# Two attention layers in fp32: layer 0 by half rows again, and an opening that loads the pair ahead of most of x

## The chip, the cores and the metric

The kernel runs on one core of a Trainium2 chip. The metric is the device time of one execution, in microseconds. The profile is of one execution of the kernel before, with a span of 3475.1 us. The engines are named as in the profile: PE (TensorE, matmuls), PEld (its weight loads), DVE (VectorE), ACT (ScalarE), POOL (GpSimd), SP (SyncE, which only issues transfers here).

## The reference, cut to what matters

x has 128 rows of 256 tokens with 256 channels. Both layers add attention to x, computed from a group-normalized x (32 groups, statistics over all rows and tokens). Layer 0 has 8 heads of 32 channels, adds a bias made from `pair` after the softmax, and multiplies by a gate. Layer 1 has 4 heads of 64 channels and sees a band of 16 tokens to each side.

```python
def layer0(x, pair, gate_proj, qkv_proj, out_proj, bias_proj):     # x: (1, 128, 256, 256)
    bias = einsum('nijz,zh->nhij', pair, bias_proj)[:, None]       # pair: (1, 256, 256, 128)
    gate = sigmoid(x @ gate_proj)
    q, k, v = split(x @ qkv_proj, 3)                               # 8 heads of 32
    sim = softmax(einsum('nsqhc,nskhc->nshqk', q, k) / sqrt(32)) + bias
    return (einsum('nshqk,nskhc->nsqhc', sim, v) * gate) @ out_proj

def layer1(x, w_in, b_in, w_out, b_out):
    q, k, v = split(x @ w_in.T + b_in, 3)                          # 4 heads of 64
    scores = where(|i - j| <= 16, q k^T / sqrt(64), -inf)
    return softmax(scores) @ v @ w_out.T + b_out

x = x + layer0(groupnorm(x), ...)
x = x + layer1(groupnorm(x), ...)
```

The statistics of the first group norm need the whole of x, so layer 0 cannot start before x has been read once. Those of the second need all of layer 0's result.

## The kernel before

All is fp32. It has three parts: an opening (weights, the bias from `pair`, the statistics of x), layer 0 row by row, and layer 1 row by row. A branch at the end recomputes everything in a slower way if a sum of exponentials was out of range; with these inputs it isn't taken.

The opening. The weights are issued on ScalarE's queue. Layer 1's weights (`w_nat`, one transfer for each of 12 blocks and one for `w_out`) are turned by TensorE ahead of everything else. Then 32 steps m, each on half a tile of `pair` (16 tiles of 2 MB, three buffers): `turn_pair` transposes it on TensorE and copies it out, `weigh_pair` multiplies it by the bias weights, `place_bias` turns the result back into `bias_sb`. x comes in parts of 4 MB (the last two of 3 and 1 MB) in two buffers; DVE counts each with 32 `bn_stats`, one for a group.

```python
for a in range(A):
    nc.scalar.dma_start(out=qkv_sb[strip(a)], in_=by_strip(qkv_w)[a])
    nc.scalar.dma_start(out=gate_sb[strip(a)], in_=by_strip(gate_w)[a])
# ... out_sb, bqk, bv, bo and the 13 transfers of w_nat alike ...
for o4 in range(2):                      # layer 1's weights, turned
    for kt in range(2):
        pw = proj_bank(...)
        for j in range(4):
            nc.tensor.transpose(pw[...], w_nat[...], ident)
        # ... nc.scalar.copy into w_in_t, w_out_t ...

steps = NM // (NX - 1)                   # NM = 32, NX = 9
for m in range(NM):
    if m % (IC // 16) == 0:
        load_pair(m // (IC // 16))       # on SyncE's queue
    turn_pair(m)
    if m >= 1: weigh_pair(m - 1)
    if m >= 2: place_bias(m - 2)
    n, k = divmod(m, steps)
    if n >= 1:
        x_stats(stats, xss[n - 1], n - 1, range(k * G // steps, (k + 1) * G // steps))
    if k == steps - 1 and n < NX - 2:
        xss[n] = x_load(xs_pool, x[0], n, "0_")   # on SyncE's queue
# ...
for n in range(NX - 2, NX):
    x_stats(stats, x_load(xs_pool, x[0], n, "0_"), n)
mean0, rstd0 = group_columns(...)
```

Layer 0. A row s has two halves of four heads. `scores` makes the four `sim` banks of a half, their exponentials `ex` and the sums over the two key tiles `both`. `piece(s, n)` normalizes a row (n = 0) or projects q, k, v or the gate (n = 1 to 4). `attend` handles all eight heads at once, between the two halves of the next row's scores. PSUM has five shared banks, and one each for zs, bv and av.

```python
def attend(s):
    # zs: sums of the exponentials, as rows of `ones`; bv: bias times v; av: ex times v
    for half, both in enumerate((both0, both1)):
        for j in range(4):
            nc.tensor.matmul(zs[D0 * j : D0 * (j + 1), half, :], lhsT=ones[:, 0:D0], rhs=both[:, j, :], ...)
    for to, weights in ((bv0, bias), (av, ex)):
        for half in range(2):
            for kt in range(2):
                for j in range(4):
                    nc.tensor.matmul(to[D0 * j : D0 * (j + 1), half, :], lhsT=v[...], rhs=weights(h, kt), ...)
    nc.scalar.activation(z, zs, AF.Identity, accum_out=zsum[:, s : s + 1])
    nc.vector.scalar_tensor_tensor(d, st[s]["e"], 1.0, z, op0=ALU.add, op1=ALU.mult)
    nc.vector.tensor_tensor(t, bv0, z, ALU.mult)
    nc.vector.tensor_tensor(t, av, t, ALU.add)
    nc.vector.reciprocal(d, d)
    nc.vector.tensor_tensor(at, t, d, ALU.mult)
    nc.vector.tensor_reduce(zmin[:, s : s + 1], z, axis=AX.XY, op=ALU.min)

def finish(s):
    po = by_channel(out_sb, 0, st[s]["at"], ...)         # 8 PE instructions
    nc.vector.tensor_tensor(o[:, k], po, st[s]["xt"], ALU.add)
    # every second row: bn_stats for layer 1; every SG = 4 rows: store to x1

for s in range(S + 1):
    if s < S: scores(s, 0)
    attend(s - 1)
    if s < S: scores(s, 1)
    for n in range(1, 5): piece(s + 1, n)
    finish(s - 1)
    piece(s + 2, 0)
```

An fp32 matmul is two PE instructions; `by_channel` and `by_token` (q, k, v, gate, out) are four matmuls of 128 x 128 by 256 columns each. Layer 1 has the same frame with its own shapes and isn't touched.

Of the kernel before, what the change touches and what calls it, by code (L numbers as in the profile page):

```python
# [9 lines left out]
F32 = mybir.dt.float32  # L10
AF = mybir.ActivationFunctionType
ALU = mybir.AluOpType
# [22 lines left out]
def conv_preact_kernel(  # L35
# [19 lines left out]
    dram = ctx.enter_context(tc.tile_pool(name="dram", bufs=1, space=bass.MemoryType.DRAM))  # L55


    ring = {}

    def psum(scope, name, proj, sim):  # L60

        pool = scope.enter_context(tc.tile_pool(name=f"ps_{name}", bufs=1, space=PSUM))
        ring["proj"] = (pool, "proj", proj)
        ring["sim"] = (pool, "sim", sim) if sim else ring["proj"]
        return pool

    def bank(which, name):
        pool, tag, bufs = ring[which]
        return pool.tile([P, 2, R], F32, tag=tag, name=name, bufs=bufs)

    def proj_bank(name):
        return bank("proj", name)

    def sim_bank(name):
        return bank("sim", name)
# [19 lines left out]
    def strip(a):  # L95
        return slice(B * a, B * (a + 1))
# [3 lines left out]
    for a in range(A):  # L100
        nc.scalar.dma_start(out=qkv_sb[strip(a)], in_=by_strip(qkv_w)[a])
        nc.scalar.dma_start(out=gate_sb[strip(a)], in_=by_strip(gate_w)[a])
    out_sb = const.tile([P, 2, C], F32, name="out_sb")
    for kt in range(2):
        for h in range(2):
            nc.scalar.dma_start(
                out=out_sb[:, kt, h * P : (h + 1) * P].rearrange("p (a r) -> p a r", a=A),
                in_=out_w.rearrange("(t p) (a h r) -> t h p a r", p=P, a=A, h=2)[kt, h],
            )
    bqk = const.tile([P, 4], F32, name="bqk")  # L110
    with nc.allow_non_contiguous_dma(reason="512 biases, once"):
        nc.scalar.dma_start(out=bqk, in_=b_in[0 : 2 * C].rearrange("(t p) -> p t", p=P))

    bv = const.tile([P, P], F32, name="bv")
    for half in range(2):
        nc.scalar.dma_start(
            out=bv[KB * half : KB * (half + 1), :],
            in_=b_in[2 * C + P * half : 2 * C + P * (half + 1)].partition_broadcast(KB),
        )
    bo = const.tile([P, 2], F32, name="bo")  # L120
    with nc.allow_non_contiguous_dma(reason="256 biases, once"):
        for a in range(A):
            nc.scalar.dma_start(out=bo[strip(a)], in_=b_out.rearrange("(a h r) -> a r h", a=A, h=2)[a])
# [31 lines left out]
    zmin = const.tile([P, 2 * S], F32, name="zmin")  # L155
    zsum = const.tile([P, 2 * S], F32, name="zsum")
# [98 lines left out]
    with ExitStack() as early:  # L255
        ps_av = psum(early, "early", 2, 4)
# [5 lines left out]
        for t in range(6):  # L262
            for h in range(2):
                nc.scalar.dma_start(
                    out=w_nat[:, t, h * P : (h + 1) * P].rearrange("p (a r) -> p a r", a=A),
                    in_=w_in.rearrange("(t p) (a h r) -> t h p a r", p=P, a=A, h=2)[t, h],
                )
        nc.scalar.dma_start(out=w_nat[:, 6:8, :], in_=w_out.rearrange("(t p) c -> p t c", p=P))
        for o4 in range(2):
            for kt in range(2):  # L270
                pw = proj_bank(f"pw{o4}_{kt}").rearrange("p a b -> p (a b)")
                for j in range(4):
                    nc.tensor.transpose(
                        pw[:, j * P : (j + 1) * P], w_nat[:, 4 * o4 + j, kt * P : (kt + 1) * P], ident
                    )
                if o4 == 0:
                    nc.scalar.copy(w_in_t[:, kt, 0:512], pw)
                else:
                    nc.scalar.copy(w_in_t[:, kt, 512:768], pw[:, 0:256])
                    for h in range(2):  # L280
                        nc.scalar.copy(
                            w_out_t[:, kt, h * P : (h + 1) * P].rearrange("p (a r) -> p a r", a=A),
                            pw[:, 256:512].rearrange("p (a h r) -> p h a r", a=A, h=2)[:, h],
                        )

# [56 lines left out]
        steps = NM // (NX - 1)  # L342
        xss = {}
        for m in range(NM):
            if m % (IC // 16) == 0:
                load_pair(m // (IC // 16))
            turn_pair(m)
            if m >= 1:
                weigh_pair(m - 1)
            if m >= 2:  # L350
                place_bias(m - 2)
            n, k = divmod(m, steps)
            if n >= 1:
                x_stats(stats, xss[n - 1], n - 1, range(k * G // steps, (k + 1) * G // steps))
            if k == steps - 1 and n < NX - 2:
                xss[n] = x_load(xs_pool, x[0], n, "0_")
        weigh_pair(NM - 1)
        place_bias(NM - 2)
        place_bias(NM - 1)
        for n in range(NX - 2, NX):  # L360
            x_stats(stats, x_load(xs_pool, x[0], n, "0_"), n)
# [29 lines left out]
    def by_channel(w, col, xn, name, ring="proj"):  # L391

        ps = bank(ring, name)
# [20 lines left out]
    SG = min(4, S)  # L414
# [8 lines left out]
    with ExitStack() as lay:  # L423
        st1 = lay.enter_context(tc.tile_pool(name="st1", bufs=1))
        stats1 = st1.tile([P, 2, S // 2, 6], F32, name="stats1")
        with ExitStack() as lay0:
            ps_av = psum(lay0, "0", 5, 0)
# [38 lines left out]
            def scores(s, half):  # L466
# [10 lines left out]
                ex = att.tile([P, 4, 2, R], F32, tag="ex", name=f"ex{s}_{half}", bufs=3)  # L477
                for j in range(4):
                    nc.scalar.activation(ex[:, j], sims[j], AF.Exp, scale=1.0 / math.sqrt(D0))  # L479
                both = att.tile([P, 4, R], F32, tag="both", name=f"both{s}_{half}", bufs=3)  # L480
# [4 lines left out]
            def attend(s):  # L485
                if s < 0:
                    return
                (ex0, both0), (ex1, both1) = hd.pop((s, 0)), hd.pop((s, 1))
                v = st[s]["v"]

                zs = ps_av.tile([P, 2, R], F32, tag="z", name=f"zs{s}")
                bv0 = ps_av.tile([P, 2, R], F32, tag="bv", name=f"bv{s}")
                av = ps_av.tile([P, 2, R], F32, tag="av", name=f"av{s}")
                for half, both in enumerate((both0, both1)):
                    for j in range(4):
                        nc.tensor.matmul(
                            zs[D0 * j : D0 * (j + 1), half, :], lhsT=ones[:, 0:D0], rhs=both[:, j, :],
                            start=True, stop=True,
                        )
                for to, weights in (  # L500
                    (bv0, lambda h, kt: bias_sb[:, kt, h, :]),
                    (av, lambda h, kt: (ex0, ex1)[h // 4][:, h % 4, kt, :]),
                ):
                    for half in range(2):
                        for kt in range(2):
                            for j in range(4):
                                h = 4 * half + j
                                nc.tensor.matmul(  # L508
                                    to[D0 * j : D0 * (j + 1), half, :],
                                    lhsT=v[:, kt, h * D0 : (h + 1) * D0], rhs=weights(h, kt),  # L510
                                    start=(kt == 0), stop=(kt == 1),
                                )
                z = att.tile([P, 2, R], F32, tag="z", name=f"z{s}")
                nc.scalar.activation(z, zs, AF.Identity, accum_out=zsum[:, s : s + 1])
                d = att.tile([P, 2, R], F32, tag="d", name=f"d{s}")
                nc.vector.scalar_tensor_tensor(d, st[s]["e"], 1.0, z, op0=ALU.add, op1=ALU.mult)
                t = att.tile([P, 2, R], F32, tag="t", name=f"t{s}")
                nc.vector.tensor_tensor(t, bv0, z, ALU.mult)
                nc.vector.tensor_tensor(t, av, t, ALU.add)
                nc.vector.reciprocal(d, d)  # L520
                at = row.tile([P, 2, R], F32, tag="at", name=f"at{s}")
                nc.vector.tensor_tensor(at, t, d, ALU.mult)  # L522
                st[s]["at"] = at
                nc.vector.tensor_reduce(zmin[:, s : s + 1], z, axis=AX.XY, op=ALU.min)  # L524
# [22 lines left out]
            for s in range(S + 1):  # L547
                if s < S:
                    scores(s, 0)
                attend(s - 1)  # L550
                if s < S:
                    scores(s, 1)
                for n in range(1, 5):
                    piece(s + 1, n)
                finish(s - 1)
                piece(s + 2, 0)
            mean1, rstd1 = channel_columns(st1, stats1, 1)
# [4 lines left out]
    with ExitStack() as lay:  # L562
        ps_av = psum(lay, "1", 2, 4)
# [91 lines left out]
        def divide(s):  # L655
# [4 lines left out]
            n = S + s  # L660
# [8 lines left out]
        def finish(s):  # L669
            if s < 0:  # L670
                return
            po = by_channel(w_out_t, 0, st[s]["at"], f"1po{s}", "sim")
# [37 lines left out]
    ps_av = psum(ctx, "2", 2, 4)  # L710
# [12 lines left out]
    with tc.If(sure < P):  # L723
        with ExitStack() as lay:
            one = lay.enter_context(tc.tile_pool(name="one2", bufs=1))
# [175 lines left out]
```

## Time and profile before

| what | value |
|---|---|
| time, median of 3 runs (range) | 3476.82 us (3476.82 to 3478.02) |
| span of the profiled execution | 3475.1 us |
| granted TensorE clock, mean | 0.982 |
| layer 0's first projection starts | 248.5 us |
| layer 1's first projection starts | 2256.4 us |
| read from HBM, written | 136.65 MB, 67.11 MB |

The three parts of the kernel are found by the starts of their first projections: the opening ends at 248.5 us, layer 0 at about 2256 us, layer 1 with the span. The page gives the busy time of every engine over the whole span, the same in 40 slices of 87 us, and groups of instructions with their mean durations. The views that show what waits for what are the trace in order of time and the table of waits. A busy PE is no proof that PE does useful work all the time, because the ends of its matmuls are modelled; the distance from one start to the next is what is measured.

### The profile page before, as it was taken

How to read it: one execution, taken by the hardware profiler on the slowest of the kernel's cores; microseconds unless marked ns; L12 is line 12 of the kernel's file. 1: busy time of each engine (PE TensorE's matmuls, PEld its weight loads, DVE VectorE, ACT ScalarE, POOL GpSimd, SP SyncE). 2: the span in 40 equal slices, each digit the busy share in tenths (PEclk: the TensorE clock that was granted, in tenths of full speed). 3: DMA queues.
4: the chain of work that ended last, by engine and by line, in shares of the span. 5: the costliest groups of instructions: out<-in, count | busy, mean ns of one | idle time of the engine just before them, and what ended most of it. 6: DMA issues, size and time to landing. Idle time of an engine off the chain costs nothing. (4 is left out here: it accounts for less than half of the span.)

```text
span 3475.1 us, 88975 instructions
## 1 busy us (share of the span) xinstructions
PE 3324.6 (96%) x39840; PEld 2617.4 (75%) x39840; DVE 2573.3 (74%) x3837; ACT 1369.2 (39%) x2927; POOL 238.5 (7%) x169
## 2 busy tenths in 40 slices
PE   4759999999999999999999999799999999999997
PEld 2547777777777777777777777588888888888886
DVE  3777777777777777777777777667777777777776
ACT  2324444444444444444444444233333333333332
POOL 0000000000000000000000000012112112112111
PEclk9879999999999999999999999899999999999998
DMA  8992121211212112121121200112222222222222
GB/s 254 353 235 34 26 50 26 37 38 25 50 26 38 38 26 50 25 38 38 25 50 26 38 26 14 53 35 71 54 50 71 54 51 71 54 51 71 54 51 39
DMA packets 361637, 209.54 MB, mean 60 GB/s; under 512 B 277280, under 2 KB 343456, under 8 KB 360096
## 3 DMA queue, kind: packets, MB, share of 16 engines
q1 hardware_dynamic: 350736, 201.35, 23.7%
q8 instruction: 314, 5.14, 0.6%
q10 hardware_dynamic: 10512, 2.43, 0.4%
q14 instruction: 75, 0.61, 0.1%
HBM read 136.65 MB, written 67.11 MB: 59 GB/s over the span
## 5 line engine op out<-in xcount | busy, mean ns | idle before, releaser
L479 ACT ACTIVATE ex<-sim 128x512 f32<-128x512 f32 x1024 | 528.7, 603 | 643.9 <-PE sim L472 643.9
L663 DVE RECIPROCAL 1rz<-1z 128x512 f32<-128x512 f32 x128 | 429.1, 3353 | 193.2 <-ACT 1z L661 193.2
L627 POOL TENSOR_TENSOR 1p<-1ex,seen 128x768 f32<-128x768 f32 x128 | 231.6, 1809 | 3206.4 <-ACT 1ex L625 3206.4
L520 DVE RECIPROCAL d<-d 128x512 f32<-128x512 f32 x128 | 427.7, 3341 | 0.0
L482 DVE TENSOR_TENSOR both<-ex 128x512 f32<-128x512 f32 x512 | 333.6, 681 | 66.2 <-ACT ex L479 66.2
L371 DVE TENSOR_SCALAR xn<-xt,mean,rstd 128x256 f32<-128x256 f32 x256 | 94.0, 409 | 276.6 <-PE pg L396 276.6
L472 PE MATMUL sim<-q,k 32*128 32x256 f32 x4096 | 294.9, 400 | 0.2 <-ACT ex L479 0.2
L472 PEld LDWEIGHTS sim<-q,k 32*128 32x128 f32 x4096 | 185.9, 184 | 101.4 <-DVE zmin L524 51.9
L396 PE MATMUL 1po<-1at,w_out_t 128*128 128x256 f32 x1024 | 258.5, 396 | 2.8 <-DVE 1at L665 2.8
L396 PE MATMUL pq<-xn,qkv_sb 128*128 128x256 f32 x1024 | 257.1, 394 | 2.0 <-issue 2.0
L588 ACT ACTIVATE 1q<-p1q,bqk 128x256 f32<-128x256 f32 x256 | 107.3, 470 | 380.6 <-PE p1q L396 380.6
L396 PE MATMUL po<-at,out_sb 128*128 128x256 f32 x1024 | 245.7, 383 | 8.1 <-DVE at L522 8.1
L596 PEld LDWEIGHTS p1v<-w_in_t,xn 128*64 128x64 f32 x4096 | 220.9, 137 | 42.4 <-issue 42.4
L596 PE MATMUL p1v<-w_in_t,xn 128*64 128x128 f32 x4096 | 251.9, 276 | 0.0
L396 PE MATMUL p1q<-xn,w_in_t 128*128 128x256 f32 x1024 | 244.0, 382 | 6.6 <-DVE xn L371 6.6
L508 PE MATMUL bv<-bias_sb,v 128*32 128x256 f32 x4096 | 244.5, 379 | 0.0
L508 PE MATMUL av<-ex,v 128*32 128x256 f32 x4096 | 244.5, 379 | 0.0
L396 PE MATMUL pk<-xn,qkv_sb 128*128 128x256 f32 x1024 | 242.9, 380 | 0.0
L396 PE MATMUL p1k<-xn,w_in_t 128*128 128x256 f32 x1024 | 242.5, 380 | 0.0
L407 PE MATMUL pv<-qkv_sb,xn 128*128 128x256 f32 x1024 | 242.0, 379 | 0.0
L396 PE MATMUL pg<-xn,gate_sb 128*128 128x256 f32 x1024 | 241.9, 379 | 0.0
L396 PEld LDWEIGHTS pq<-xn,qkv_sb 128*128 128x128 f32 x1024 | 185.2, 191 | 64.4 <-issue 44.2
(118 smaller groups left out, 4864.9 us busy)
## 6 DMA issues: line engine op xcount, KB each, us to landing
xg<-in_x_dram SPq DMA_DIRECT2D x128, 256.0 KB, 5.8
x<-o SPq DMA_DIRECT2D x32, 1024.0 KB, 4.6
yg<-x SPq DMA_DIRECT2D x32, 1024.0 KB, 5.7
out_dram<-1o SPq DMA_DIRECT2D x128, 256.0 KB, 6.3
xs<-in_x_dram SPq DMA_DIRECT2D x7, 4096.0 KB, 20.8
xs<-in_x_dram SPq DMA_DIRECT2D x1, 3072.0 KB, 19.1
xs<-in_x_dram SPq DMA_DIRECT2D x1, 1024.0 KB, 10.5
qkv_sb<-in_L_conv_qkv_proj_dram ACTq DMA_DIRECT2D x4, 192.0 KB, 7.4
```

The costliest lines, as they stand in the source:

```text
L371: nc.vector.tensor_scalar(xn[:, half, :], xt[:, half, :], mean[:, half : half + 1], rstd[:, half : half + 1], op0=ALU.subtract, op1=ALU.mult,)
L396: nc.tensor.matmul(ps[:, m, :], lhsT=w[:, kt, col + m * P : col + (m + 1) * P], rhs=xn[:, kt, :], start=(kt == 0), stop=(kt == 1),)
L407: nc.tensor.matmul(ps[:, t, :], lhsT=a[:, kt, t * P : (t + 1) * P], rhs=w[:, kt, col : col + C], start=(kt == 0), stop=(kt == 1),)
L472: nc.tensor.matmul(sims[j][:, kt, :], lhsT=k[p0 : p0 + D0, half, kt * P : (kt + 1) * P], rhs=q[p0 : p0 + D0, half, :], start=True, stop=True,)
L479: nc.scalar.activation(ex[:, j], sims[j], AF.Exp, scale=1.0 / math.sqrt(D0))
L482: nc.vector.tensor_tensor(both[:, j : j + 2], ex[:, j : j + 2, 0, :], ex[:, j : j + 2, 1, :], ALU.add)
L508: nc.tensor.matmul(to[D0 * j : D0 * (j + 1), half, :], lhsT=v[:, kt, h * D0 : (h + 1) * D0], rhs=weights(h, kt), start=(kt == 0), stop=(kt ...
L520: nc.vector.reciprocal(d, d)
L588: nc.scalar.activation(a[:, half, :], ps[:, half, :], AF.Identity, bias=b)
L596: nc.tensor.matmul(ps[KB * half : KB * (half + 1), b, :], lhsT=xn[:, kt, KB * b : KB * (b + 1)], rhs=w_in_t[:, kt, 2 * C + P * half : 2 * ...
L627: nc.gpsimd.tensor_tensor(p.rearrange("p j b q -> p j (b q)"), ex.rearrange("p j b q -> p j (b q)"), seen.rearrange("p b q -> p (b q)").un ...
L663: nc.vector.reciprocal(rz, z)
```

## The change

It has two parts. In the opening, the weights are issued from GpSimd's queue instead of ScalarE's (only the small bias weights stay there). Layer 1's weights are turned after a quarter of the pair steps (m = 8) and no longer ahead of them. Four parts of x are loaded amid the pair (at m = 4, 12, 20 and 28), the other five after it. The purpose is that the pair doesn't wait for the weights and that the queue is busy from the start.

In layer 0, `attend` works on a half row and is called in every half step; the whole-row form, which stood in this kernel, goes. The half step is: scores of a half, two or three projections, attention of the half before. The order of av, bv and z on TensorE changes with it, `ex` and `both` have two buffers instead of three, and the store of x1 goes by 8 rows instead of 4. PSUM has two projection banks and four score banks for the whole kernel, and one each for avz and bv0.

```diff
-        nc.scalar.dma_start(out=qkv_sb[strip(a)], in_=by_strip(qkv_w)[a])
-        nc.scalar.dma_start(out=gate_sb[strip(a)], in_=by_strip(gate_w)[a])
+        nc.gpsimd.dma_start(out=qkv_sb[strip(a)], in_=by_strip(qkv_w)[a])
+        nc.gpsimd.dma_start(out=gate_sb[strip(a)], in_=by_strip(gate_w)[a])
 ... out_sb, bqk, bv, bo, w_nat alike; the turning of w_nat becomes turn_weights() ...
-        steps = NM // (NX - 1)
-        xss = {}
+        early_x = {NM * (2 * n + 1) // 8: n for n in range(4) if n < NX - 2}
+        xss, to_count = {}, []
         for m in range(NM):
 ...
-            n, k = divmod(m, steps)
-            if n >= 1:
-                x_stats(stats, xss[n - 1], n - 1, range(k * G // steps, (k + 1) * G // steps))
-            if k == steps - 1 and n < NX - 2:
+            if m == NM // 4:
+                turn_weights()
+            if m in early_x:
+                n = early_x[m]
                 xss[n] = x_load(xs_pool, x[0], n, "0_")
+                to_count += [(m + 4, n, g) for g in range(G)]
+            for _ in range(6):
+                if to_count and to_count[0][0] <= m:
+                    _, n, g = to_count.pop(0)
+                    x_stats(stats, xss[n], n, [g])
 ...
-        for n in range(NX - 2, NX):
-            x_stats(stats, x_load(xs_pool, x[0], n, "0_"), n)
+        for n in range(NX):
+            if n in xss:
+                x_stats(stats, xss[n], n, [g for _, k, g in to_count if k == n])
+            else:
+                x_stats(stats, x_load(xs_pool, x[0], n, "0_"), n)
 ...
-    SG = min(4, S)
+    SG = min(8, S)
 ...
-            def attend(s):
+            def attend(s, half):
+                ex, both = hd.pop((s, half))
+                avz = ps_av.tile([P, 2, R], F32, tag="avz", ...)
+                bv0 = ps_av.tile([P, R], F32, tag="bv0", ...)
+                for kt in range(2):
+                    for j in range(4):
+                        nc.tensor.matmul(avz[ps, 0, :], lhsT=v[:, kt, ch], rhs=ex[:, j, kt, :], ...)
+                for kt in range(2):
+                    for j in range(4):
+                        nc.tensor.matmul(bv0[ps, :], lhsT=v[:, kt, ch], rhs=bias_sb[:, kt, 4 * half + j, :], ...)
+                for j in range(4):
+                    nc.tensor.matmul(avz[ps, 1, :], lhsT=ones[:, 0:D0], rhs=both[:, j, :], ...)
+                nc.scalar.activation(z, avz[:, 1, :], AF.Identity, accum_out=zsum[:, n : n + 1])
+                nc.vector.tensor_tensor(t, bv0, z, ALU.mult)
+                nc.vector.tensor_tensor(t, avz[:, 0, :], t, ALU.add)
+                nc.vector.scalar_tensor_tensor(d, st[s]["e"][:, half, :], 1.0, z, op0=ALU.add, op1=ALU.mult)
+                nc.vector.reciprocal(d, d)
+                nc.vector.tensor_tensor(st[s]["at"][:, half, :], t, d, ALU.mult)
+                nc.vector.tensor_reduce(zmin[:, n : n + 1], z, axis=AX.X, op=ALU.min)
 ...
-            for s in range(S + 1):
-                if s < S:
-                    scores(s, 0)
-                attend(s - 1)
-                if s < S:
-                    scores(s, 1)
-                for n in range(1, 5):
-                    piece(s + 1, n)
-                finish(s - 1)
-                piece(s + 2, 0)
+            n_steps = 2 * S
+            for i in range(n_steps + 2):
+                s, half = divmod(i, 2)
+                if i < n_steps:
+                    scores(s, half)
+                if half == 0:
+                    piece(s + 1, 1)
+                    piece(s + 1, 2)
+                    piece(s + 2, 0)
+                else:
+                    piece(s + 1, 3)
+                    piece(s + 1, 4)
+                    finish(s - 1)
+                if 0 <= i - 1 < n_steps:
+                    attend(*divmod(i - 1, 2))
```

## The prediction

> **What bounds the kernel now.** I read the page's busy totals first, then the 40 slices, then the order of time on PE inside one row of layer 0, then the opening on PE, on the DMA queue and on DVE.
>
> ```profile
> PE 3324.6 (96%) x39840; PEld 2617.4 (75%) x39840; DVE 2573.3 (74%) x3837; ACT 1369.2 (39%) x2927; POOL 238.5 (7%) x169
> PE   4759999999999999999999999799999999999997
> DMA  8992121211212112121121200112222222222222
> ```
>
> PE is full from the fourth slice (87 us each) to the end. Only the opening (slices one to three) and the seam between the layers leave it idle. So the time is an opening that PE does not set, plus 128 rows of layer 0, plus 128 rows of layer 1, each row costing what PE takes. Layer 1's code is untouched, so two places matter: the row of layer 0 and the opening. One row of layer 0 in order of time, PE alone:
>
> ```profile
> 1000.36 1.15 PE L472 MATMUL sim<-q,k 32*128 32x256 f32 x16
> 1001.43 2.00 PE L396 MATMUL pq<-xn,qkv_sb 128*128 128x256 f32 x8
> 1003.26 1.89 PE L396 MATMUL pk<-xn,qkv_sb 128*128 128x256 f32 x8
> 1004.99 1.89 PE L407 MATMUL pv<-qkv_sb,xn 128*128 128x256 f32 x8
> 1006.72 1.89 PE L396 MATMUL pg<-xn,gate_sb 128*128 128x256 f32 x8
> 1008.45 1.89 PE L396 MATMUL po<-at,out_sb 128*128 128x256 f32 x8
> 1010.26 1.15 PE L472 MATMUL sim<-q,k 32*128 32x256 f32 x16
> 1011.34 1.07 PE L496 MATMUL zs<-both,ones 128*32 128x256 f32 x16
> 1012.23 1.91 PE L508 MATMUL bv<-bias_sb,v 128*32 128x256 f32 x32
> 1013.96 1.91 PE L508 MATMUL av<-ex,v 128*32 128x256 f32 x32
> 1015.79 1.15 PE L472 MATMUL sim<-q,k 32*128 32x256 f32 x16
> ```
>
> The first column is the start. Ends are modelled and overlap, so only starts are compared. From sim to the same sim one row later: 1015.79 - 1000.36 = 15.43 us. pk, pv and pg each take 1.73 us from start to start for 8 instructions: 0.216 us for one 256-column pass, which I call a slot. The narrow matmuls (32 rows or 32 columns of the array) run four side by side, so sim is 4 slots, zs 4, bv 8, av 8. The row holds 5 x 8 + 2 x 4 + 4 + 8 + 8 = 68 slots = 14.69 us. The remaining 0.74 us sits where the shape changes: pq takes 1.83 instead of 1.73, the two sims 1.07 and 1.08 instead of 0.86, po 1.81, av 1.83, zs 0.89. By seams: av to sim 0.21, sim to pq 0.21, po to sim 0.20, sim to zs 0.13. Nothing else waits.
>
> Now the opening: two stages of 20 us, one line of the DMA queue's waits, and two lines in order of time.
>
> ```profile
> 20.00:40.00 20.00, 1.45 (x4) 0.57 (x4) 3.25 (x8) 0.00 (x0) 0.00 (x0) 1.00 0.80 260
> 40.00:60.00 20.00, 9.76 (x43) 5.92 (x44) 2.05 (x4) 6.37 (x14) 0.00 (x0) 1.00 0.59 141
> SPq L296 <- DMA w_nat<-in_L_conv_w_in_dram: 23.7, 1, 23.7
> 52.22 0.47 PE L273 MATMUL pw<-ident,w_nat 128*128 128x128 f32 x1 [5.55 <-DMA w_nat<-in_L_conv_w_in_dram]
> 226.29 12.44 DVE L252 BATCH_NORM_STATS2 stats<-xs 128x6 f32<-128x192 f32 x64
> ```
>
> The last figure of a stage is GB/s. From 60 us to 220 us the queue moves 328 to 358 GB/s, so the opening is a DMA stage; but for the first 60 us it moves 246, 260 and 141. PE stands before layer 1's weights (w_nat), which land late, so the pair's tiles aren't turned, their three buffers stay full, and the third pair load is held. At the far end the last two parts of x are counted by DVE from 226.29 to 238.75, the group constants follow, and layer 0's first projection starts at 248.5.
>
> **What the Trainium skill says.** "TensorEngine Tiling (Array Packing)", Key Properties: changing the tiling mode drains TensorE, changing the tile alone doesn't. This trace agrees: every seam of the row that changes mode costs 0.13 to 0.21 us, and zs to bv, bv to av, pk to pv (same mode) cost nothing. "DMA: Bandwidth & Descriptors", SWDGE vs HWDGE vs iDMA: a transfer issued by GpSimd has its descriptors made by software there, one issued by ScalarE or SyncE by hardware; the section on issuing engines adds that all end on the same 16 DMA engines. The kernel before has no GpSimd transfer, so its trace cannot show the former; the latter agrees, since the queue of the weights and the queue of the pair share the first 60 us.
>
> **The change part by part.**
>
> *Layer 0 goes back to half rows.* The slots stay: av, bv and z are the same matmuls, 68 a row. What changes is the order. By the order of instructions, a row becomes two steps: sim, pq, pk, av, bv, z of the other half; then sim, pv, pg, po, av, bv, z. Each step has three changes of mode, six a row in place of four: sim to projection twice, z to sim twice, projection to av twice. The first two kinds cost 0.21 each in the row above. For the third (whole array to column strips) I take layer 1, where p1k to p1v is such a seam:
>
> ```profile
> 2302.43 1.89 PE L396 MATMUL p1k<-xn,w_in_t 128*128 128x256 f32 x8
> 2304.25 1.97 PE L596 MATMUL p1v<-w_in_t,xn 128*64 128x128 f32 x32
> ```
>
> 1.82 us instead of 1.73: 0.09, plus some 0.03 on the first strip (as zs showed) = 0.12. So 4 x 0.21 + 2 x 0.12 = 1.08 us a row against 0.74: +0.34, and x 128 = **+43 us**.
>
> Does a half step stall? The tight place is po. It needs the second half of `at`, from the z that ended just ahead of the step's sim. On PE, sim (1.07), pv (1.83) and pg (1.73) lie between, and po's third instruction is the first to read that half: 1.07 + 1.83 + 1.73 + 0.43 = 5.06 us. The chain: z on ScalarE with its accumulator read, about 0.6 (half of a 0.63 us instruction plus 0.24, overlapping); then on DVE three of about 0.35 (half of 0.68), the reciprocal about 1.7 (half of 3.34), zmin 0.35, at 0.4 = 3.5; with 0.2 of hand-over 4.3 us. It fits with 0.7 to spare. The single PSUM banks of avz and bv0 are read out about 1.9 us after z; the next av starts 4.7 us after it. DVE's load per row rises from about 11.6 us (75% of 15.43) to about 12.3 through smaller instructions, ScalarE's hardly: both below 15.8. So no stall: 15.77 us a row.
>
> *The weights leave ScalarE's queue, and PE turns them after a quarter of the pair.* The queue need not stop at 20 to 60 us. In the first 60 us the kernel before moved 20 x (246 + 260 + 141) = 12.9 MB where 350 GB/s would give 21. That hole is 8 MB, or 23 us at 350 GB/s, but the 10512 small packets of the weights still take 5.2% of the 262 us opening, 13.6 us, wherever they are issued; I count them. New opening: start 2, weights 13.6, the pair (33.6 MB) and seven 4 MB parts of x (29.4 MB) at 347 GB/s 181.5, small gaps in the tail 1.5 = 198.6 us when the seventh part lands.
>
> *Most of x comes after the pair.* Five parts are then counted with nothing beside them. DVE takes 0.33 us for one of 32 groups (18 in 5.96 us in this trace), 10.7 us a part, and the queue 12.1 us, so the queue still leads and DVE follows. From the seventh part: 10.7 + 12.4 for the last two parts (they took 12.44 above) = 221.7 us. Before it was 238.75: **-17 us**.
>
> *The seam.* The store of x1 goes by 8 rows instead of 4, so the last one carries 1 MB more, +3 us before layer 1 can load; in return the last row's attention needs only half a row after the last exponentials, about -3 us. Zero.
>
> Sum: 3476.8 + 43 - 17 + 0 = **3503 us**.
>
> **The rivals.**
> 1. *The opening decides.* If mode changes hid under something, layer 0 would stay at 15.43 and only -17 would remain: 3460. Against it: PE has no gap in the row to hide them in.
> 2. *GpSimd's weights come late.* If software descriptors are slow, w_nat lands after PE reaches it (at about 55 us: four and a half pair tiles and a part of x loaded), PE stands again, and after about 20 us of buffers the queue stops too. The gain shrinks to nothing: about 3520. For it: 32 transfers, 16 of them in 128-byte pieces; nothing in this trace prices them.
> 3. *A new wait at po.* If the chain runs 0.3 us past its 5.06 us, 0.3 x 128 = 38 us come on top: about 3541. Against it: the 0.7 us margin.
> 4. *DVE blocks the pair.* The order shows 26 counts of a part of x ahead of the next pair copy, so DVE may stand for a part not yet landed. The kernel before has the same bunches and still ran at 345 GB/s; a loss of 5 us at most.
>
> **Range and chances.** The seam cost is read directly; its doubt (0.12 may be 0.09 to 0.16, and the schedule) is about 10 us either way. The opening may bring 0 to 25. A stall at po is the one large risk, upward. So 3480 to 3530 holds it 8 times in 10. Over 2% slower starts at 3546 and needs rivals 2 and 3 together, or a bigger stall: 0.04. Over 2% faster, 3407, would need a gain for which there is no place: 0.01.
>
> **What would show it.** In the changed profile: sim to sim over a row 15.77 us, with six short seams and no idle of PE behind `at`; layer 0's first pq near 231 us; GB/s above 300 from the first slice; w_nat not in PE's waits. The prediction is wrong if a row takes 15.43 or over 16.0, or if PE waits for w_nat for more than a few us.

## The result, and the profile after

| | before | after |
|---|---|---|
| time, median (range) | 3476.82 us (3476.76 to 3478.02) | 3506.74 us (3506.40 to 3506.87) |
| ratio to before, 95% interval | | 1.0085 [1.0068, 1.0103] |
| span of the profiled execution | 3475.1 us | 3505.0 us |
| layer 0's first projection starts (pq) | 248.56 us | 241.12 us |
| layer 1's first projection starts (p1q) | 2256.44 us | 2286.77 us |

The kernel became 30 us slower; 3503 was predicted. The three starts cut the difference of the spans, 29.9 us, into parts: the opening -7.4 us, layer 0 +37.8 us (2045.65 against 2007.88), layer 1 -0.4 us. On the page of the changed kernel TensorE's slices are as full as they were:

```profile
PE 3353.4 (96%) x39840; PEld 2586.1 (74%) x39840; DVE 2595.4 (74%) x4605; ACT 1403.9 (40%) x3183; POOL 259.7 (7%) x201
...
PE   6739999999999999999999999899999999999997
...
DMA  9980220210211112121021110022322322212222
```

PE has the same 39840 instructions as before, and it is full from the fourth slice on again: no new wait of any size in layer 0. The first two slices are fuller (6 and 7 where they were 4 and 7; DMA 9 and 9 where it was 8 and 9), the third is emptier (3 for 5). So the start of the opening got denser and its end got thinner. One row of layer 0, in order of time on PE (start, duration, instruction; only starts are compared):

```profile
1002.89 1.15 PE L474 MATMUL sim<-q,k 32*128 32x256 f32 x16
1003.97 2.00 PE L398 MATMUL pq<-xn,qkv_sb 128*128 128x256 f32 x8
1005.80 1.89 PE L398 MATMUL pk<-xn,qkv_sb 128*128 128x256 f32 x8
1007.62 1.07 PE L499 MATMUL avz<-ex,v 128*32 128x256 f32 x16
1008.50 1.05 PE L506 MATMUL bv<-bias_sb,v 128*32 128x256 f32 x16
1009.37 0.61 PE L512 MATMUL avz<-both,ones 128*32 128x256 f32 x8
1009.91 1.15 PE L474 MATMUL sim<-q,k 32*128 32x256 f32 x16
1010.99 1.99 PE L409 MATMUL pv<-qkv_sb,xn 128*128 128x256 f32 x8
1012.82 1.89 PE L398 MATMUL pg<-xn,gate_sb 128*128 128x256 f32 x8
1014.55 1.89 PE L398 MATMUL po<-at,out_sb 128*128 128x256 f32 x8
1016.37 1.07 PE L499 MATMUL avz<-ex,v 128*32 128x256 f32 x16
1017.25 1.05 PE L506 MATMUL bv<-bias_sb,v 128*32 128x256 f32 x16
1018.12 0.61 PE L512 MATMUL avz<-both,ones 128*32 128x256 f32 x8
1018.66 1.15 PE L474 MATMUL sim<-q,k 32*128 32x256 f32 x16
```

Sim to sim is 1018.66 - 1002.89 = 15.77 us, where the row before took 15.43. No line carries a bracket with a wait, po included. All six seams are to be seen, each spread over the lines on its two sides: the sims take 1.08 instead of 0.86 from start to start, pq and pv behind them 1.83 instead of 1.73, pk and po ahead of the column strips 1.82 instead of 1.73, and z ahead of sim 0.54 instead of 0.43.

The opening, by the DMA view of the first 235 us. This line gives GB/s in 40 slices of 5.9 us:

```profile
GB/s 154 237 233 233 285 299 377 333 257 289 290 291 291 414 402 285 290 291 291 350 402 352 290 290 290 291 405 396 303 404 402 363 357 245 409 375 222 178 0 95
```

The hole of the kernel before (its stages had 260 and 141 GB/s at 20 to 60 us) is gone. Three levels are left: 233 to 237 while the first weights pass, 285 to 291 while only the pair is loaded, and 350 to 414 in most of the slices with a part of x. In the last quarter the figures fall off. What DVE does there, in order of time (a bracket says how long it stood, and for what):

```profile
184.95 20.97 DVE L243 BATCH_NORM_STATS2 stats<-xs 128x6 f32<-128x256 f32 x64
208.12 22.90 DVE L243 BATCH_NORM_STATS2 stats<-xs 128x6 f32<-128x256 f32 x96 [2.20 <-DMA xs<-in_x_dram]
```

From 184.95 to 231.02 us DVE does nothing but count the last five parts of x: the fifth and sixth, a wait of 2.2 us for the seventh, then three more. The table of waits says who stands for it:

```profile
PE ps_m L172 <- DVE means L162: 48.4, 1, 48.4
...
SPq L237 <- DVE stats L243: 42.7, 4, 11.2
```

PE stands for 48.4 us in one piece for the constants. SyncE's queue stands four times, 42.7 us in all, before it may issue the next part of x: there are two buffers for x, and both are full of tokens not yet counted. w_nat isn't in PE's waits at all.

### The profile page after: what moved, and what is told of

Its sections match the earlier page's. It is cut to its first block, busy times and chain, and to the rows that moved or that the text cites. A ratio compares the mean times of both kernels' runs of the same rounds, so it can differ in the third digit from the quotient of the medians.

```text
span 3505.0 us, 90352 instructions
## 1 busy us (share of the span) xinstructions
PE 3353.4 (96%) x39840; PEld 2586.1 (74%) x39840; DVE 2595.4 (74%) x4605; ACT 1403.9 (40%) x3183; POOL 259.7 (7%) x201
## 3 DMA queue, kind: packets, MB, share of 16 engines
q1 hardware_dynamic: 350480, 201.35, 23.6%
q0 software_dynamic: 1136, 2.43, 0.3%
## 5 line engine op out<-in xcount | busy, mean ns | idle before, releaser
L523 DVE RECIPROCAL d<-d 128x256 f32<-128x256 f32 x256 | 445.8, 1742 | 0.0
L519 DVE TENSOR_TENSOR t<-bv,z 128x256 f32<-128x256 f32 x256 | 108.6, 424 | 417.9 <-ACT z L517 417.9
L517 ACT ACTIVATE z<-avz 128x256 f32<-128x256 f32 x256 | 98.1, 383 | 679.8 <-PE avz L512 668.6
L499 PE MATMUL avz<-ex,v 128*32 128x256 f32 x4096 | 275.7, 386 | 1.2 <-DVE t L520 1.2
L506 PE MATMUL bv<-bias_sb,v 128*32 128x256 f32 x4096 | 269.7, 380 | 1.1 <-DVE t L519 1.1
L409 PE MATMUL pv<-qkv_sb,xn 128*128 128x256 f32 x1024 | 255.2, 392 | 0.0
## 6 DMA issues: line engine op xcount, KB each, us to landing
xs<-in_x_dram SPq DMA_DIRECT2D x1, 3072.0 KB, 10.7
```

What stands on the lines that cost most here:

```text
L409: nc.tensor.matmul(ps[:, t, :], lhsT=a[:, kt, t * P : (t + 1) * P], rhs=w[:, kt, col : col + C], start=(kt == 0), stop=(kt == 1),)
L499: nc.tensor.matmul(avz[ps, 0, :], lhsT=v[:, kt, ch], rhs=ex[:, j, kt, :], start=(kt == 0), stop=(kt == 1),)
L506: nc.tensor.matmul(bv0[ps, :], lhsT=v[:, kt, ch], rhs=bias_sb[:, kt, 4 * half + j, :], start=(kt == 0), stop=(kt == 1),)
```

## The experiments

The theory after reading this: the slowdown is the row's two extra changes of mode and nothing else, the opening gives only 7 us because x counted after the pair lies in the open, and the two parts don't touch each other. The rivals: half-width instructions or single PSUM banks cost the row its 0.34 us; the opening's end is set by the queue; the parts interact. All ratios are against the kernel before as it ran beside each experiment (median 3477.65 us for 1 to 4, 3477.94 for 5 to 9), with 95% intervals; differences in us are taken from the 3476.82 of the table above.

**1. The new opening alone**, on whole rows:

```diff
 # kernel before, plus the weights on GpSimd's queue, turn_weights() at m == NM // 4,
 # and the four early parts of x; layer 0, PSUM and SG as before
+        early_x = {NM * (2 * n + 1) // 8: n for n in range(4) if n < NX - 2}
```

> The new opening with the whole-row layer 0 of the kernel before. If the two parts of the change act separately, the time is that of before less what the opening gained in the changed kernel's trace (first projection at 241.1 us instead of 248.5): about 3469 us, with a row of layer 0 at 15.43 us. If the opening's gain needs the half rows, or is eaten later, it stays near 3477 us.

Measured: 3467.26 us (3464.65 to 3468.20), ratio 0.9970 [0.9958, 0.9982]. The row takes 15.44 us, pq starts at 240.7, p1q at 2246.3.

**2. The half rows alone**, behind the old opening:

```diff
 # changed kernel, with ScalarE's queue, w_nat turned first and x's order as before
-        early_x = {NM * (2 * n + 1) // 8: n for n in range(4) if n < NX - 2}
+        steps = NM // (NX - 1)
```

> The old opening with the half-row layer 0 (and its stores by 8 rows). Separate parts: 3476.8 + 37.8 (layer 0 from its first projection to layer 1's first: 2007.9 us before, 2045.7 after) = about 3514 us, first projection again near 248.5 us, a row at 15.77 us. If half rows cost less than that on their own, 3490 us or lower.

Measured: 3515.84 us (3514.39 to 3516.82), ratio 1.0110 [1.0094, 1.0125]. The row takes 15.77 us, pq starts at 250.1, p1q at 2295.9. The parts add up: the opening moves the median by -9.6 with whole rows (3467.26 - 3476.82) and -9.1 with half rows (3506.74 - 3515.84); the half rows by +39.0 and +39.5.

**3. One more change of mode in whole rows.** No instruction, no bank and no buffer changes: one projection moves up into the gap between sim and zs, which turns four seams into five.

```diff
                     scores(s, 0)
+                piece(s + 1, 1)
                 attend(s - 1)
                 if s < S:
                     scores(s, 1)
-                for n in range(1, 5):
+                for n in range(2, 5):
                     piece(s + 1, n)
```

> The kernel before, with the q projection moved between the first scores and the attention: whole rows, same banks, same instructions, but five changes of mode in a row instead of four (sim to projection 0.21 and projection to strips 0.12 in place of sim to zs 0.13, so +0.20 us). Theory of the seams: a row at 15.63 us and +26 us in all, about 3503 us. Rival, that the half rows cost time through smaller instructions or their single banks: nothing changes, 3477 us.

Measured: 3501.58 us (3500.50 to 3502.78), ratio 1.0070 [1.0054, 1.0085]. The same view as above, of this kernel:

```profile
1004.09 1.15 PE L472 MATMUL sim<-q,k 32*128 32x256 f32 x16
1005.17 1.99 PE L396 MATMUL pq<-xn,qkv_sb 128*128 128x256 f32 x8
1007.09 1.07 PE L496 MATMUL zs<-both,ones 128*32 128x256 f32 x16
...
1019.73 1.15 PE L472 MATMUL sim<-q,k 32*128 32x256 f32 x16
```

Sim to sim is 1019.73 - 1004.09 = 15.64 us against 15.43: about 0.2 us a row, some 26 us in 128 rows; the times differ by 24.8. The seam sim to zs went, and sim to pq and pq to zs came: from pq's start to that of zs it is 1.92 us, where pk, pv and pg took 1.73. Whole rows with whole banks pay the same kind of money, so half-width instructions and single banks aren't needed to explain the half rows.

**4 to 6. The opening taken apart**, on the kernel before, with x in its old order. Fourth: the weights on GpSimd's queue and turned at m = 8. Fifth: only the queue. Sixth: only the late turn.

```diff
-        nc.scalar.dma_start(out=qkv_sb[strip(a)], in_=by_strip(qkv_w)[a])     # 4 and 5,
+        nc.gpsimd.dma_start(out=qkv_sb[strip(a)], in_=by_strip(qkv_w)[a])     # and all weights alike
+            if m == NM // 4:                                                  # 4 and 6
+                turn_weights()
```

> The kernel before with the weights on GpSimd's queue and turned at step 8, but x spread over the whole pair as before: the new opening without its x order. If the tail of five parts counted by DVE alone is what keeps the new opening from gaining more, this one gains more: first projection near 232 us, about 3460 us. If the order of x is what brings the gain, the first projection stays at 245 us or later, about 3474 us.

> The kernel before with the weights issued by GpSimd and nothing else: TensorE still turns layer 1's weights first. In the changed kernel the last of these transfers is issued at 40.4 us and takes 12.3 us to land, as late as in the kernel before. So TensorE should stand until about 53 us again and the time stay: 3474 to 3478 us. If it is ScalarE's issuing that held the opening, the gain of 13 us of the kernel with both parts comes already here: about 3465 us.

> The kernel before with layer 1's weights turned at step 8, still issued on ScalarE's queue. ScalarE's order holds all its transfers ahead of its first pair copy, and the last was issued at 44.2 us in the kernel before, so the pair stands until about 45 us for want of ScalarE's copies instead of until 53 us for the weights: a part of the gain, 3470 to 3474 us. If the wait for the weights on TensorE is all that mattered, 3465 us.

| | time (range) | ratio | pq starts |
|---|---|---|---|
| 4: queue and late turn | 3464.71 us (3463.40 to 3466.18) | 0.9963 [0.9950, 0.9977] | 236.7 |
| 5: queue only | 3465.16 us (3464.05 to 3465.85) | 0.9965 [0.9951, 0.9979] | 236.2 |
| 6: late turn only | 3468.47 us (3467.23 to 3469.32) | 0.9973 [0.9963, 0.9983] | 240.6 |

Four brought less than expected, five against my expectation the whole of it, and six a little more than expected. Either edit alone takes most of the 12 us, so there were two holds, one behind the other.

The first is TensorE's turning. TensorE goes on with the pair when it has turned w_nat; in the kernel before:

```profile
54.66 1.75 PE L309 MATMUL pz<-ident,pr 128*128 128x128 f32 x8
```

In the sixth run, with the weights still on ScalarE's queue, it goes on 8.1 us sooner:

```profile
46.59 2.82 PE L310 MATMUL pz<-ident,pr 128*128 128x128 f32 x12 [27.82 <-ACT prt L313]
```

The first buffer of the pair comes free that much sooner (the fourth load is issued at 49.5 us and not at 58.5), and pq starts 8.0 us sooner. The second hold, worth the other 4 us, goes with ScalarE's queue. SyncE's issues in order of time, of the fifth run:

```profile
7.81 14.62 SPq L246 DMA_DIRECT2D xs<-in_x_dram  x1
22.64 21.07 SPq L296 DMA_DIRECT2D pr<-in_L_conv_pair_repr_dram  x2
```

The third load of the pair is issued at 22.64 us; in the kernel before it was issued at 41.20, and in the sixth run at 41.21:

```profile
41.21 8.99 SPq L297 DMA_DIRECT2D pr<-in_L_conv_pair_repr_dram  x2
```

The waits of the sixth run say why:

```profile
SPq L297 <- DMA w_nat<-in_L_conv_w_in_dram: 23.9, 2, 23.6
...
PE pz L310 <- ACT prt L313: 27.8, 1, 27.8
```

With the weights on ScalarE's queue SyncE stands 23.6 us for a transfer of w_nat, whether TensorE turns w_nat early or late; and TensorE stands 27.8 us for ScalarE's first copy of the pair, because ScalarE is busy issuing weights until 44.6 us. I had put the whole hole down to TensorE's turning. In the fifth run TensorE still waits for w_nat (10.6 us), and the time is that of the fourth. But that run isn't the queue alone: in its trace TensorE does 48 transposes of the pair ahead of w_nat, where the kernel before has 16.

**7. Is that wait made by the order of the program's text?** The third load has a free buffer from the start. In the built program it waits for a semaphore of an earlier transfer, one of eight that SyncE's and ScalarE's transfers take in turn, last taken by a block of w_nat; with GpSimd's queue that wait isn't in the program.

```diff
+        load_pair(0); load_pair(1)
+        xss = {0: x_load(xs_pool, x[0], 0, "0_")}
+        load_pair(2)
         w_nat = st_pool.tile([P, 8, C], F32, name="w_nat")
```

> The kernel before with one thing moved: the first three loads of the pair and the first part of x stand ahead of layer 1's weights in the program's text, on the same queue and in the same order among themselves; the weights stay on ScalarE's queue and are turned first. In the kernel before the third pair load stands at 41.2 us, in SyncE's waits behind a transfer of w_nat that ScalarE issued, though its buffer was free from the start. If that wait is only the bookkeeping of transfers (a load takes the semaphore of an earlier transfer of another engine, in the order of the program's text), it vanishes here: the third pair load is issued by about 23 us as in the run with GpSimd's queue, the queue fills some 2 to 3 MB of its hole, 7 to 10 us, and the kernel takes 3467 to 3471 us; not all 13 us of the run with GpSimd's queue, because ScalarE is still busy issuing until 44 us and the fourth load waits for its copies. If the load waits for the hardware behind the weights' transfers instead, it stays near 41 us and the time at 3475 to 3478.

Measured: 3478.18 us (3476.05 to 3480.11), ratio 1.0001 [0.9993, 1.0009]. The waits of this run:

```profile
SPq L270 <- DMA w_nat<-in_L_conv_w_in_dram: 24.0, 1, 24.0
```

The load is issued at 42.47 us, and the wait is where it was. This edit didn't take the wait out of the built program (it still names the same semaphore), so it tells only that the order of the text doesn't decide it. That the wait is one of the program and not of the transfer hardware rests on the program's list of waits and on the fifth run. "DMA: Bandwidth & Descriptors" of the Trainium skill, Anatomy of one DMA (its section is on GpSimd's transfers), says that DMA engines don't wait for semaphores and that such a wait happens on the issuing engine before dispatch. This trace agrees: it is SyncE that stands, 24.0 us. No run here takes this wait away and leaves the weights with ScalarE.

**8. The end of the opening: queue or DVE?** The changed kernel, with the five late parts counted over half of their tokens. This leaves half of those tokens out of the statistics; the loads stay.

```diff
-    def x_stats(stats, xs, n, groups=range(G)):
-        k = PARTS[n]
+    def x_stats(stats, xs, n, groups=range(G), part=1):
+        k = PARTS[n] // part
 ...
-                x_stats(stats, x_load(xs_pool, x[0], n, "0_"), n)
+                x_stats(stats, x_load(xs_pool, x[0], n, "0_"), n, part=2)
```

> The changed kernel, with the five parts of x that come after the pair counted on half of their tokens; this leaves out half of these tokens from the statistics. If DVE's counting bounds the tail (parts at 10.5 us each on DVE with two buffers, the queue idle in between), the queue takes over at some 400 GB/s and the first projection comes 8 to 12 us sooner: about 3496 us. If the queue bounds the tail, nothing changes: 3507 us.

Measured: 3496.86 us (3496.42 to 3497.55), ratio 1.0056 [1.0041, 1.0071], 9.9 us less than the changed kernel; pq starts at 230.3. DVE in order of time:

```profile
183.91 6.28 DVE L243 BATCH_NORM_STATS2 stats<-xs 128x6 f32<-128x128 f32 x32
194.00 6.28 DVE L243 BATCH_NORM_STATS2 stats<-xs 128x6 f32<-128x128 f32 x32 [3.81 <-DMA xs<-in_x_dram]
204.99 6.28 DVE L243 BATCH_NORM_STATS2 stats<-xs 128x6 f32<-128x128 f32 x32 [4.72 <-DMA xs<-in_x_dram]
212.27 8.19 DVE L243 BATCH_NORM_STATS2 stats<-xs 128x6 f32<-128x96 f32 x64 [1.00 <-DMA xs<-in_x_dram]
```

A part takes 6.28 us, and DVE now stands before the sixth, the seventh and the eighth. So this shows when the queue can deliver: the sixth part at 194.0, the seventh at 205.0, the eighth at 212.3. In the changed kernel DVE started on the seventh at 208.12 and ended at 231.02. The counts end at 212.27 + 8.19 = 220.46, 10.6 us sooner. Of these, 1.0 is not the edit's: DVE starts on the fifth part at 183.91 and not at 184.95. Another 2.1 came because the seventh part landed sooner, and 7.4 because the counting after that took 15.5 us and not 22.9. The end of the changed kernel's opening is DVE's and not the queue's.

**9. All of x amid the pair**, on run 4's kernel: one part every three pair steps (NM // NX), so that x ends before the pair does.

```diff
-        steps = NM // (NX - 1)
+        steps = NM // NX
 ...
-            if k == steps - 1 and n < NX - 2:
+            if k == steps - 1 and n < NX:
                 xss[n] = x_load(xs_pool, x[0], n, "0_")
 ...
-        for n in range(NX - 2, NX):
-            x_stats(stats, x_load(xs_pool, x[0], n, "0_"), n)
```

> The kernel before with the weights on GpSimd's queue, turned at step 8, and all nine parts of x loaded amid the pair, so that the last two tiles of the pair come last. The queue should end at about 211 us as in the run with the weights' part alone, and no counting of x is left after it (12.4 us there); the last pair steps take some 8 us and the group constants lie beside them. First projection near 224 us instead of 236.7, about 3452 us. If the queue loses by the order, or the counting only holds the pair up, 3460 us or more.

Measured: 3455.44 us (3454.54 to 3457.80), ratio 0.9937 [0.9923, 0.9951]: faster than both kernels. pq starts at 228.8. The last groups of x are counted from 210.09 us on, amid the pair, so no counting is left behind it:

```profile
210.09 0.34 DVE L252 BATCH_NORM_STATS2 stats<-xs 128x6 f32<-128x64 f32 x2
...
217.05 0.69 DVE L315 COPY prt<-pz 128x512 f32<-128x512 f32 x1 [2.96 <-PE pz L310]
...
226.05 0.51 DVE L338 COPY bias_sb<-pbt 128x32 f32<-128x32 f32 x4
```

DVE stands 2.96 us for the pair's transposes ahead of 217.05, and then does the pair's last copies and the rest of the constants in turn. The last copy of the pair, at 226.05, comes just ahead of the last steps of the constants. So the opening now ends with the pair's work.

## Why the prediction held, point by point

**The row: right.** 15.77 predicted, 15.77 measured, with the six seams where they were put and nothing behind po. So rival 1, a row that stays at 15.43, fell. From the second row's first sim to the last row's (269.31 to 2214.32 before, 261.62 to 2248.85 after, 126 rows) layer 0 grew by 42.2 us; 43 was put down for 128. That seams are the cause was an argument in the prediction; run 3 shows it, since it adds one seam and no instruction. "TensorEngine Tiling (Array Packing)", Key Properties, says that a change of tiling mode drains TensorE; runs 2 and 3 agree and give the price that the page doesn't: in the half rows six changes cost 1.08 us a row above its 68 slots (15.77 - 14.69), 0.18 each on the average. The split by kinds, 0.12 to 0.21, is the prediction's reading; the runs bear out its sums.

**Rivals 2, 3 and 4: fallen.** GpSimd's weights weren't late. w_nat was turned at 69.75 us without a wait, its last issue having ended at 41 us. And PE waits for `at` only in the last rows, 4.9 us in all; in the kernel before it was 8.1. DVE stood 5.8 us in all for parts of x, 2.2 of them behind the pair, so it hardly held the pair up.

**The seam between the layers: 0 predicted, about -4 measured.** From the last row's first sim to p1q it was 42.1 us before and 37.9 after. The half-row tail gave all of it: from that sim to the issue of the last store it was 28.3 us before and 24.3 after, -4 where -3 was put down. The store's +3 wasn't there, though the store does take longer (the page gives 7.7 us for 2 MB, and 4.6 us for 1 MB before). Before, the load of layer 1 waited for its store and then still 3.2 us for DVE's constants; after, the two come at the same time:

```profile
SPq L580 <- DMA x<-o: 7.0, 1, 7.0
```

SyncE issues the load 7.75 us after the store in the changed kernel and 7.74 us after it in the kernel before. The term was a real duration, but a hidden one.

**The opening: -17 predicted, -7.4 measured by pq's start (-9.6 and -9.1 in the medians, by runs 1 and 2). This is the step that failed.** It had the seventh part of x landing at 198.6 us, and 23.1 us of counting after it. The counting was right: 22.90 us. The landing was wrong: DVE got the part at 208.1. Two of the signs failed with it: pq starts at 241.1 us and not near 231, and the first slice of the page shows 291 GB/s and not over 300. Two terms were mis-sized.
- The rate, some 6 to 7 of these 9.5 us. Run 8, where DVE holds nothing back, has the seventh part at 205.0 us, or 206.0 without its head start of 1.0. The 347 GB/s came from stages in which two loads of the pair went with each part of x. By the rates of the changed kernel's slices it is a mean of two, the pair at 290 and x at about 410 (4.2 MB / 290 + 4.2 MB / 410 is 24.7 us for 8.4 MB, 340 GB/s), and by the seventh part the new order has loaded more of the slow kind. An estimate with these two rates and the prediction's other terms gives 2 + 13.6 + 33.6 MB / 290 + 29.4 MB / 410 + 1.5 = 204.7 us. It leans on the rate of x, which isn't steady (350 to 439 GB/s here), so the split is good to a few us.
- The buffers, 2 to 3: 208.1 against 206.0 or 205.0. I had written that the queue, at 12.1 us a part, leads at the end and that DVE follows at 10.7. In run 8 a part came 11.0 us after the one before, so the lead is small, and with two buffers it is lost: the seventh part goes where the fifth was, and its load can start only when DVE has counted that one. It is issued at 195.5 us.

The order of x is thus a loss of its own, and the prediction had it as a gain. By its figures the filled hole was worth 23 - 13.6 = 9.4 us and the order had to bring the other 7.6. Measured by the starts of pq, the weights' part brought 11.9 us (248.6 to 236.7, run 4), and the order took 4.0 back (236.7 to 240.7, run 1), of which 2.7 are left at the first scores (246.6 and 249.3). In the times this is 3464.71 against 3467.26 us, whose ranges overlap; run 9, which goes the other way with x, gains 9.3 us on run 4, with ranges far apart, and bears out the direction.

**Why the hole was there: in part right.** That the queue stops because the weights come late was right, and so was TensorE's standing before w_nat: turning them late was worth 8.0 us (run 6). That this wait holds the third pair load was wrong. That load had a free buffer and stood 23.7 us in SyncE's queue for a w_nat transfer. And behind TensorE's wait stood ScalarE's 44 us of issuing. These two cost the other 4 us (run 4); what each of them cost alone is not shown.

That the sum was close is in part luck, because the errors were opposed: the opening was put 9.6 us too good and layer 0 5.2 us too bad (43 against 37.8), and layer 1 ran 0.4 us faster. They leave some 30 us in place of 26.

## What to carry to other kernels

Where TensorE is full, count the changes of tiling mode in a row and group the narrow matmuls; each one cost 0.1 to 0.2 us here, and two more in 128 rows ate four times what a better opening brought. A mean transfer rate holds only for the mix that it was read from: when an order changes, price each kind of transfer by its own stretch. Put work that another engine must count or turn amid the transfers that leave that engine idle, not behind them, and don't issue dozens of weights from an engine whose copies the first tiles need.

## What the runs showed of the hardware that was not expected

- The rate depended on what was loaded: 285 to 291 GB/s for the pair (512-byte pieces), 439 GB/s for x in the stage from 185 to 190 us. "DMA: Bandwidth & Descriptors", Specifications, gives 512 bytes as the smallest piece at full rate and about 358 GB/s as one core's share of HBM; in this trace 512 bytes didn't reach the rate of x's long pieces, and x, with one core at work, went past that share. The pair and x differ in their layout too, so it isn't shown that the length of the piece is the cause. These are the stages of the changed kernel (columns: stretch, length, busy time of PE, PEld, DVE, ACT, POOL, granted clock, DMA share, GB/s); in the third the queue is all but empty while DVE counts:

```profile
60.00:68.00 8.00, 8.00 (x51) 6.38 (x50) 5.14 (x11) 3.02 (x7) 0.00 (x0) 0.77 1.05 290
...
185.00:190.00 5.00, 0.00 (x0) 0.00 (x0) 5.00 (x17) 0.00 (x0) 0.00 (x0) 0.65 1.02 439
...
215.00:220.00 5.00, 0.00 (x0) 0.00 (x0) 5.00 (x18) 0.00 (x0) 0.00 (x0) 0.50 0.15 29
```

- The same 2.43 MB of weights went as 1136 packets from GpSimd's queue and as 10512 from ScalarE's. On GpSimd's queue they took 4.7% of the first 235 us, 11.0 us, where the prediction put 13.6. An issue took GpSimd 0.54 to 0.77 us whatever its shape; on ScalarE the four of out_sb took 9.7 us and the 512 single biases 5.0 us.
- Issuing engine by pattern, on the same page, calls transfers issued by SyncE and ScalarE generally faster. Here the move of the weights from ScalarE to GpSimd gained 11.7 us (run 5): with it went ScalarE's 44 us of issuing, and SyncE's wait for a w_nat transfer.
